# A four-layer graph network on one core: layer 2's feed-forward computed for all rows in small steps, instead of for packed rows in one stage

## The chip, the core and the metric

The kernel is written in Bass with the Tile framework and runs on one core of a Trainium2 chip. The metric is the device time of one execution in microseconds (us). A core has engines that run side by side, each with a queue of its own that it works off in order: PE (TensorE, matrix products; its weight loads are shown as PEld), DVE (VectorE), ACT (ScalarE), POOL (GpSimd) and SP (SyncE, which issues most DMA transfers). They wait for one another through semaphores. Which instruction stands where in a queue is fixed when the kernel is built.

## What is computed

3125 nodes with 256 features and 50,000 edges go through four layers. Each adds a graph convolution and a mixing block to the rows, and then a feed-forward block. The change concerns layer 2's feed-forward, what stands before it and what follows it:

```python
x = x + L2_gnn(xn, edge_index, ...) + L2_mix(xn[None], ...)[0]   # attention with 8 heads; linear attention
x = x + L2_ffn(_layernorm(x)[None], ...)[0]
xn = _layernorm(x)
x = x + L3_gnn(xn, ..., edge_index) + L3_mix(xn[None], ...)[0]

def L2_ffn(x, wr, br, w1, b1, w2, b2):            # b = 1, s = 3125
    weights = (jnp.einsum('bsd,do->bso', x, wr) + br)[..., 0]
    k = max(1, int(0.5 * s)); kk = k - 1          # kk = 1561
    _, idx = jax.lax.top_k(weights, k)
    sel_idx = idx[:, :kk]
    sel = jnp.take_along_axis(x, sel_idx[:, :, None], axis=1)
    h = jax.nn.gelu(jnp.einsum('bkd,dh->bkh', sel, w1) + b1, approximate=True)   # 256 -> 1024
    y = jnp.einsum('bkh,hd->bkd', h, w2) + b2                                    # 1024 -> 256
    y = y * jnp.take_along_axis(weights, sel_idx, axis=1)[..., None]
    return jnp.zeros_like(x).at[batch_idx, sel_idx].set(y) + x
```

So each row gets a weight; the 1561 rows with the largest weights are kept; only they go through the feed-forward, whose result is multiplied with the weight and added.

## The kernel before

The rows are held on chip as `x`, 25 tiles of 128 rows (`NB = 25`), handled in groups of `BB = 5` tiles. Most of the kernel is emitted through Tile, whose pools decide when a buffer is free again; the order on each queue is the order in which the Python code emits.

*End of layer 2's attention* (`gat`, from L906). For each group of five tiles: scale by the softmax sums, add the bias (L917), statistics (`stats`: L441 and L442 on DVE, a square root at L444 on ACT), shift and scale (L922, five Identity activations on ACT), multiply with `gamma` (L923), add to `x` (L924).

*Feed-forward* (`ffn2`). The weights `w1` and `w2` (1024 KB each) are loaded. `norm_x` normalises all groups; its `each` copies the normed rows to `xn_all` (L1784) and makes each row's weight `wt` (L1787). A search over the bits of the weights follows: eight rounds of four bits, each with a comparison on DVE (L1833), a count (L1835), a sum over partitions on PE (L1837) and a choice. From its threshold come `sel`, the kept rows, `cw`, the factor of each row, and by three prefix sums (`before`, L1856 and L1857) the place `ids` of each kept row and the place `back` where each row finds its result. Then 25 indirect DMAs on POOL write every tile's rows to their places in DRAM (`kept`, L1890). The first 13 tiles of it, `KS`, are the kept rows: SP loads them (`xs`, L1903), PE transposes them (`to_T`, L456, copied by ACT or DVE at L457), and the feed-forward runs in groups of four tiles: eight chunks of 128 hidden features (`feat`, L502, 512 columns; gelu on ACT, L1913), then for each tile the second product (`tok`, L465, with the bias at L463), a copy (L1918) and a store to DRAM (`done`, L1919). Last, 25 indirect DMAs on POOL gather each row's result (`yb`, L1923), and DVE adds it times `cw` to `x` (L1926).

*Layer 3* (`layer3`, `dense3`). After the index set-up of its mixture of experts, the kernel reads a flag (`unfit`) and takes, for these inputs, `dense3`: norm by groups, and in `first` the normed rows times `di` are split into three bf16 parts `ha` by casts on ACT (L2139) and subtractions on DVE (L2141). The graph product is then, for each of 25 blocks of destinations, 75 products of `ha` with a matrix of edge counts (`product`, L2154). The first of them needs the last `ha`.

`layer2`, `ffn2` and `layer3` follow one another in the list of layers in `tile_gps`; `xT`, the transposed rows, is one buffer up to layer 2 and another in layer 3.

Of the kernel before, what the change touches and what calls it, by code (L numbers as in the profile page):

```python
# [19 lines left out]
P = 128  # L20
N = 3125
D = 256
# [18 lines left out]
NR = 40  # L41
RB = 4
# [22 lines left out]
class Net:  # L65
# [671 lines left out]
    def gat(self, pool, pre, H, tiny, side, deg=None, after=None, during=None):  # L737
# [169 lines left out]
        then = after() if after is not None else None  # L907
        for b in range(0, NB, BB):
            s = slice(b, b + BB)
            if H > 4 or b < 2 * BB:  # L910
                nc.vector.tensor_tensor(heads[:, s], heads[:, s], bc(ws[:, s], [None, None, None, C]), ALU.mult)
            else:
                for t in range(b, b + BB):
                    for h in range(H):
                        nc.scalar.mul(heads[:, t, h, :], heads[:, t, h, :], ws[:, t, h:h + 1])
            o = agg[:, s, :D]
            nc.vector.tensor_tensor(o, o, bc(bias, [None, BB, None]), ALU.add)  # L917
            mv, rs = self.stats(pool, lambda i: agg[:, b + i, :D], BB, "gat")
            off = pool.tile([P, BB], F32, name="off")
            nc.vector.scalar_tensor_tensor(off, mv[:, :, 0], -1.0, rs, op0=ALU.mult, op1=ALU.mult)  # L920
            for i in range(BB):
                nc.scalar.activation(o[:, i, :], o[:, i, :], AF.Identity, bias=off[:, i:i + 1], scale=rs[:, i:i + 1])  # L922
            nc.vector.tensor_tensor(o, o, bc(gamma, [None, BB, None]), ALU.mult)  # L923
            nc.vector.tensor_tensor(self.x[:, s], self.x[:, s], o, ALU.add)  # L924
            if then is not None:
                then(b)
# [379 lines left out]
    def mixture(self, whole, mark, pre, names, kind, gate, gate_b, H, act, twice=False, affine=None):  # L1306
# [103 lines left out]
        def rest():  # L1410
# [8 lines left out]
            with self.pool("own_ps", 1, PSUM) as few:  # L1419
# [26 lines left out]
                place = p.tile([1, ES], F32, name="place")  # L1446
# [147 lines left out]
    def layer0(self):  # L1594
        with ExitStack() as whole:
            rest = []

            def after():
# [5 lines left out]
                return lambda b: all(True for _ in route(b))  # L1604
# [152 lines left out]
    def layer2(self):  # L1757
        nc, tc = self.nc, self.tc
        self.norm_x()
        with self.pool("mix", 1) as mw:  # L1760
            with self.pool("gnn", 1) as gw, self.pool("gnn2", 2) as gp:
                self.gat(Pools(gw, gp, GAT_ONE), "L2_gnn_", 8, 0.0, lambda own: self.mix2(mw, own))

    def ffn2(self):
# [3 lines left out]
        KS = -(-keep // P)  # L1768
        pre = "L2_ffn_"
        done = self.dram.tile([KS * P, D], F32, name="done")  # L1770
        kept = self.dram.tile([(KS + NB) * P, D], F32, name="kept")
        with self.pool("kept", 1) as p:
            w1, w2 = self.weight(p, pre + "w1"), self.weight(p, pre + "w2")
            b1, b2 = self.plain(p, pre + "b1"), self.three_of(p, pre + "b2")
            xn_all = p.tile([P, NB, D], F32, name="xn_all")

            none = p.tile([P, D], F32, name="none")
            nc.vector.memset(none, 0.0)
            nc.sync.dma_start(kept[(KS - 1) * P:KS * P], none)
            wt = p.tile([P, NB], F32, name="wt")  # L1780
            wr, br = self.rows(p, pre + "wr"), self.rows(p, pre + "br")

            def each(lp, ps, b, xn):
                nc.scalar.copy(xn_all[:, b:b + BB, :], xn)  # L1784
                for i in range(BB):
                    junk = lp.tile([P, D], F32, name="junk")
                    nc.vector.scalar_tensor_tensor(junk, xn[:, i, :], 1.0, wr, op0=ALU.mult, op1=ALU.mult,  # L1787
                                                   accum_out=wt[:, b + i:b + i + 1])

            self.norm_x(keep_xn=True, each=each, turn=False)  # L1790
            nc.vector.tensor_scalar(wt, wt, br, None, op0=ALU.add)

            wk = p.tile([P, NB], F32, name="wk")
# [4 lines left out]

            ids = p.tile([P, NB], I32, name="ids")
            back = p.tile([P, NB], I32, name="backs")  # L1800
            cw = p.tile([P, NB], F32, name="cw")
            with self.pool("rk", 1) as r, self.pool("rk2", 2) as r2, \
                    self.pool("rk_ps", 2, PSUM) as ps:
# [23 lines left out]
                for sh in range(28, -4, -4):  # L1827
# [8 lines left out]
                    q = ps.tile([P, nd], F32, name="q")  # L1836
                    nc.tensor.matmul(q, self.ones, n, start=True, stop=True)  # L1837
                    d = r2.tile([P, nd], F32, name="d")
# [14 lines left out]
                def before(x, name):  # L1853

                    q = ps.tile([P, 2, NB], F32, name="qb")
                    nc.tensor.matmul(q[:, 0], self.earlier, x, start=True, stop=True)  # L1856
                    nc.tensor.matmul(q[:, 1], self.ones, x, start=True, stop=True)  # L1857
                    t = r.tile([P, NB], F32, name=name + "t")
                    nc.vector.tensor_copy(t, q[:, 1])
                    one = r.tile([P, NB], F32, name=name + "o")  # L1860
                    nc.vector.memset(one, 0.0)
                    run = r.tile([P, NB], F32, name=name + "r")
                    nc.vector.tensor_tensor_scan(run, t, one, 0.0, ALU.add, ALU.add)
                    pl = r.tile([P, NB], F32, name=name + "p")
                    nc.vector.tensor_tensor(pl, run, t, ALU.subtract)
                    nc.vector.tensor_tensor(pl, pl, q[:, 0], ALU.add)
                    return pl, run[:, NB - 1:]

                _, larger = before(both[:, 0], "l")
                place, _ = before(both[:, 1], "e")  # L1870
                want = r.tile([P, 1], F32, name="want")
                nc.vector.tensor_scalar(want, larger, -1.0, float(keep), op0=ALU.mult, op1=ALU.add)
# [3 lines left out]
                nc.vector.tensor_tensor(cw, sel, wt, ALU.mult)  # L1876
                place, _ = before(sel, "s")

                at = r.tile([P, NB], F32, name="at")
                nc.vector.tensor_tensor(at, place, sel, ALU.mult)  # L1880
                nc.vector.tensor_copy(back, at)
                node = r.tile([P, NB], F32, name="node")
                nc.gpsimd.iota(node, pattern=[[P, NB]], base=KS * P, channel_multiplier=1,
                               allow_small_or_imprecise_dtypes=True)
                nc.vector.tensor_tensor(place, place, node, ALU.subtract)
                nc.vector.tensor_tensor(place, place, sel, ALU.mult)
                nc.vector.tensor_tensor(place, place, node, ALU.add)
                nc.vector.tensor_copy(ids, place)
            for t in range(NB):
                s = nc.gpsimd.indirect_dma_start(  # L1890
                    out=kept, out_offset=bass.IndirectOffsetOnAxis(ap=ids[:, t:t + 1], axis=0),
                    in_=xn_all[:, t, :], in_offset=None)
                if t:
                    tc.declare_no_dep(s.ins, group=pre, reason="every row has a place of its own")
                tc.add_to_no_dep_group(pre, s.ins)

            with self.pool("ks", 1) as k1, self.pool("ks2", 2) as k2, \
                    self.pool("ks_ps", 2, PSUM) as ps:
                xs = k1.tile([P, KS, D], F32, name="xs")
                sT = k1.tile([P, 2, KS * P], F32, name="sT")  # L1900
                for t0 in range(0, KS, 4):
                    n = min(4, KS - t0)
                    nc.sync.dma_start(xs[:, t0:t0 + n, :],  # L1903
                                      kept[t0 * P:(t0 + n) * P].rearrange("(t p) f -> p t f", p=P))
                    for t in range(t0, t0 + n):
                        self.to_T(ps, xs[:, t, :], sT[:, :, t * P:(t + 1) * P])
                for t0 in range(0, KS, 4):
                    n = min(4, KS - t0)
                    h = k2.tile([P, 8, 512], F32, name="h")
                    for c in range(8):  # L1910
                        q = ps.tile([P, 512], F32, name="h")[:, :n * P]
                        self.feat(q, sT, t0 * P, n * P, w1, c * P)
                        nc.scalar.activation(h[:, c, :n * P], q, AF.Gelu_apprx_tanh, bias=b1[:, c:c + 1])  # L1913
                    y = k2.tile([P, 4, D], F32, name="y")
                    for i in range(n):
                        q = ps.tile([P, D], F32, name="y")
                        self.tok(q, h, i, w2, bias=b2)
                        nc.vector.tensor_copy(y[:, i, :], q)  # L1918
                    nc.sync.dma_start(done[t0 * P:(t0 + n) * P].rearrange("(t p) f -> p t f", p=P), y[:, :n, :])  # L1919
            with self.pool("co", 8) as g:  # L1920
                for t in range(NB):
# [525 lines left out]
```

## Time and profile before

| | |
|---|---|
| median of three runs | 6186.31 us (6184.32 to 6188.53) |
| the profiled execution | 6189.69 us, span 6187.9 us |
| mean granted clock of PE | 0.862 |
| PE busy | 4643.9 us (75%) |
| DVE busy | 3297.2 us (53%) |
| ACT busy | 1567.8 us (25%) |
| POOL busy | 2397.0 us (39%) |
| end of layer 2's attention to the scatter | 4182.3 to 4301.8 us |
| scatter, packed feed-forward, gather | 4301.8 to 4476.8 us |
| layer 3's norm, to the first product with the last `ha` | 4476.8 to 4527.0 us |

The profile records one execution. The span is the time between its first and last recorded instruction; the rest of the execution's own time, some 2 us, lies around it. Busy shares of the engines overlap, so they don't add up to the span. A clock of 1.00 is full speed of TensorE; the share granted is given for each stretch of time.

### The profile page before, as it was taken

The page shows a single profiled execution, that of the slowest core. Times are in us where ns is not written, and L with a number is a line of the kernel's source. Part 1 is how long each engine was busy: PE and PEld are TensorE (multiplying, and loading weights), DVE is VectorE, ACT ScalarE, POOL GpSimd, SP SyncE. Part 2 cuts the span into 40 slices and gives each one's busy share as a digit, 9 for nine tenths or more (in the row PEclk, how much of TensorE's full clock was granted, in tenths as well). Part 3 has the DMA queues.
Part 4 walks back from the last instruction along what each step waited for, and adds up shares of the span by engine and source line. Part 5 has one row for each costly group of instructions (what it writes and reads, how often), then busy time and mean ns, then how long its engine had stood idle before and what let it go on. Part 6 is the DMA issues. An engine that isn't in the chain of part 4 may idle for free.

```text
span 6187.9 us, 81932 instructions
## 1 busy us (share of the span) xinstructions
PE 4643.9 (75%) x25310; PEld 3283.6 (53%) x25310; DVE 3297.2 (53%) x8633; ACT 1567.8 (25%) x4108; POOL 2397.0 (39%) x2340
## 2 busy tenths in 40 slices
PE   1848775696778766656697758880699999997997
PEld 1314343583565344443683235550456888786996
DVE  6448777426798388876326567776142100134222
ACT  1213233222100245432222123311144201111332
POOL 1537774322777275552423567771100000011111
PEclk9969887797897777777798879995899999998998
DMA  2744442553333144332564324430111322124554
GB/s 82 220 122 117 118 120 66 179 177 102 93 97 102 55 151 137 130 117 66 160 184 131 99 72 123 120 116 27 57 62 65 131 99 73 59 96 153 182 172 160
DMA packets 385095, 710.60 MB, mean 115 GB/s; under 512 B 100817, under 2 KB 223256, under 8 KB 384652
## 3 DMA queue, kind: packets, MB, share of 16 engines
q1 hardware_dynamic: 266431, 425.79, 21.6%
q0 software_dynamic: 108064, 269.63, 14.9%
q10 hardware_dynamic: 10157, 9.80, 0.5%
q8 instruction: 213, 3.49, 0.2%
q14 instruction: 230, 1.88, 0.1%
HBM read 571.51 MB, written 133.47 MB: 114 GB/s over the span
## 4 chain that ended last, share of the span: by engine, by line
PE 43%; issue 17%; DVE 15%; POOL 11%; DMA 8%; ACT 3%; DVEq 2%; SPq 1%; ACTq 0%; another core or an unknown queue 0%; POOLq 0%
PE dn L2154 13%; PE mm L465 6%; POOL msg L531 6%; PE g L585 4%; PE g L862 3%; DMA msg<-L_gnn_htab,src 2%; PE h L1507 2%; PE y L1520 2%; DVE ohd L2085 2%; POOL ase L531 2%; DVE agg L544 2%; DMA terms<-outr 2%; POOL back L1524 1%; PE mm L2214 1%; PE mm L2098 1%
## 5 line engine op out<-in xcount | busy, mean ns | idle before, releaser
L531 POOL DMA_INDIRECT msg<-L_gnn_c_tab,src x832 | 827.4, 995 | 606.6 <-issue 225.3
L531 POOL DMA_INDIRECT msg<-L_gnn_htab,src x832 | 887.5, 1067 | 383.5 <-issue 213.0
L544 DVE TENSOR_TENSOR agg<-agg,g 128x256 f32 (+2 forms) x1664 | 697.6, 419 | 215.0 <-PE g L862 96.3
L2154 PEld LDWEIGHTS <-a 128*128 128x128 bf16 x7500 | 736.2, 98 | 116.9 <-issue 28.3
L862 PE MATMUL g<-msg,oh 128*128 128x261 f32 (+1 forms) x1664 | 568.7, 450 | 194.0 <-DVE agg L544 176.5
L1402 POOL DMA_INDIRECT sent<-xs,ids x150 | 153.0, 1020 | 1292.9 <-DMA yb<-done,backs 1036.3
L585 PE MATMUL g<-msg,oh 128*128 128x256 f32 x1664 | 581.6, 484 | 86.5 <-DMA msg<-L_gnn_c_tab,src 35.5
L862 PEld LDWEIGHTS g<-msg,oh 128*128 128x128 f32 x1664 | 314.2, 211 | 433.6 <-DVE agg L544 328.2
L585 PEld LDWEIGHTS g<-msg,oh 128*128 128x128 f32 x1664 | 358.5, 238 | 235.4 <-DVE oh L566 86.8
L1524 POOL DMA_INDIRECT back<-y,toi x168 | 163.6, 974 | 787.1 <-DVE y L1523 510.6
L1507 PE MATMUL h<-xe,w 128*128 128x128 f32 x3584 | 436.8, 278 | 5.3 <-DMA w<-in_L_ffn_W 5.2
L2154 PE MATMUL dn<-ha,a 128*128 128x256 bf16 x3750 | 428.5, 275 | 7.7 <-ACT ha L2139 6.5
L1520 PE MATMUL y<-w,hT 128*128 x1792 | 431.2, 388 | 0.0
L1511 ACT ACTIVATE hT<-h,br 128x128 f32<-128x128 f32 x896 | 256.4, 369 | 669.5 <-issue 573.4
L1507 PEld LDWEIGHTS h<-xe,w 128*128 128x128 f32 x3584 | 422.0, 195 | 7.0 <-DVE toi L1496 6.2
L2154 PE MATMUL dn<-hb,a 128*128 128x256 bf16 x3750 | 418.2, 273 | 0.0
L1520 PEld LDWEIGHTS y<-w,hT 128*128 128x128 f32 x1792 | 326.5, 190 | 57.0
L1523 DVE COPY y<-y 128x256 f32<-128x256 f32 x168 | 71.2, 424 | 521.7 <-PE y L1520 521.5
L851 DVE TENSOR_TENSOR msg<-msg,alpha 128x1024 f32<-128x1024 f32 x208 | 254.1, 1222 | 133.4 <-DMA msg<-L_gnn_htab,src 119.9
L819 ACT COPY stage<-dm 128x24 bf16 (+1 forms) x832 | 182.5, 220 | 452.1 <-PE pd L825 281.6
L531 POOL DMA_INDIRECT ase<-tab,src x208 | 231.8, 1115 | 148.4 <-PE q L657 85.3
L566 DVE TENSOR_SCALAR oh<-cols,dl,ew 128x128 f32<-128x128 f32 x832 | 266.6, 350 | 0.0
(730 smaller groups left out, 7155.0 us busy)
## 6 DMA issues: line engine op xcount, KB each, us to landing
a<-counted SPq DMA_DIRECT2D x100, 800.0 KB
w<-in_L_ffn_W SPq DMA_DIRECT2D x128, 512.0 KB
w<-in_L_ffn_W SPq DMA_DIRECT2D x64, 1024.0 KB
counted<-T SPq DMA_DIRECT2D x40, 800.0 KB
dr<-dl_rows SPq DMA_DIRECT2D x104, 256.0 KB
sent<-zeros SPq DMA_DIRECT2D x25, 1040.0 KB
xr<-sent SPq DMA_DIRECT2D x168, 130.0 KB
lw<-lo_rows SPq DMA_DIRECT2D x78, 256.0 KB
```

Source lines behind the costliest of these rows:

```text
L465: nc.tensor.matmul(q, xT[:, k, t * P:(t + 1) * P], w[:, k, cols], start=(k == 0 and bias is None), stop=(k == nk - 1))
L531: self.nc.gpsimd.indirect_dma_start(out=out, out_offset=None, in_=table, in_offset=bass.IndirectOffsetOnAxis(ap=self.src[:, t:t + 1], axis=0))
L544: self.nc.vector.tensor_tensor(at, at, q, ALU.add)
L566: nc.vector.tensor_scalar(oh[:, j, :], self.cols, self.dl[:, t:t + 1], self.ew[:, t:t + 1], op0=ALU.is_equal, op1=ALU.mult)
L585: self.nc.tensor.matmul(r, oh[:, j, :], msg[j], start=True, stop=True)
L851: nc.vector.tensor_tensor(mh, mh, bc(al_, [None, None, None, C]), ALU.mult)
L862: nc.tensor.matmul(q, oh[:, j, :], msg[:, j, :], start=True, stop=True)
L1507: nc.tensor.matmul(q[:, i, :], d["w1"][:, k, c * P:(c + 1) * P], d["xe"][:, k, :], start=(k == 0), stop=(k == 1))
L1511: nc.scalar.activation(hT[:, c, :], q[:, i, :], act, bias=d["br"][:, c:c + 1])
L1520: nc.tensor.matmul(q, d["hT"][:, c, :], w2f[:, bass.ds(e * (nh * D) + c * D, D)], start=False, stop=(c == nh - 1))
L1524: s = nc.gpsimd.indirect_dma_start(out=self.back, out_offset=bass.IndirectOffsetOnAxis(ap=d["to"][:, 0:1], axis=0), in_=y, in_offset=None)
L2154: nc.tensor.matmul(q, a[:, k, :], h[:, k, i, :], start=(k == 0 and i == 0), stop=(k == NB - 1 and i == 2))
```

## The change

The feed-forward is no longer a stage between a packing and an unpacking of rows. It is made for all 25 tiles (25 x 128 rows instead of 13 x 128), from the transposed rows `xT`, and the result of a row that isn't kept is multiplied by a factor of zero (`f_cw`). The work is a Python generator, `forward()`, which emits one small step whenever it is asked to: for a pair of tiles four steps of two chunks of hidden features (256 columns each, gelu over 128x256 on ACT), then one step for each tile's second product.

- *The first 14 tiles* (`FIRST`) are emitted from `between()`: four calls in each group of the attention's end, two in each group of the norm, which now follows its attention group directly (`each(b)`), and two in each round of the search. What is left of them comes after the last round. Their results are copied by ACT to `ys`, and added once `f_cw` is known (`add_kept`).
- *The last 11 tiles* are emitted by `later()` within layer 3's norm, 6, 6, 6, 18 and 0 steps behind its five groups, with the weights loaded a second time; their results are added from PSUM.
- The scatter, `xs`, the transposes of packed rows, `done` and the gather go, with the prefix sum that gave the places. The transposes of layer 3's rows move out of its norm and behind the steps of their group, since the steps still read `xT`. `xT` is one buffer for the whole kernel.
- The index set-up of layer 3's mixture moves ahead of layer 2. The loads of the first feed-forward weights move ahead of the attention's end.

The core of the diff (pools and the like are left out, and the removed code that stands in the listing above):

```diff
+FIRST = 14
+PAIRS = [(t, 2) for t in range(0, 24, 2)] + [(24, 1)]
...
-        then = after() if after is not None else None
+        then, between = after() if after is not None else (None, None)
+        between = between or (lambda: None)
...
+            between()
             nc.vector.tensor_tensor(o, o, bc(bias, [None, BB, None]), ALU.add)
             mv, rs = self.stats(pool, lambda i: agg[:, b + i, :D], BB, "gat")
             off = pool.tile([P, BB], F32, name="off")
             nc.vector.scalar_tensor_tensor(off, mv[:, :, 0], -1.0, rs, op0=ALU.mult, op1=ALU.mult)
             for i in range(BB):
                 nc.scalar.activation(o[:, i, :], o[:, i, :], AF.Identity, bias=off[:, i:i + 1], scale=rs[:, i:i + 1])
+            between()
             nc.vector.tensor_tensor(o, o, bc(gamma, [None, BB, None]), ALU.mult)
+            between()
             nc.vector.tensor_tensor(self.x[:, s], self.x[:, s], o, ALU.add)
+            between()
             if then is not None:
...
     def layer2(self):
-        nc, tc = self.nc, self.tc
+
         self.norm_x()
-        with self.pool("mix", 1) as mw:
-            with self.pool("gnn", 1) as gw, self.pool("gnn2", 2) as gp:
-                self.gat(Pools(gw, gp, GAT_ONE), "L2_gnn_", 8, 0.0, lambda own: self.mix2(mw, own))
-
-    def ffn2(self):
+        with ExitStack() as whole:
+            then = []
+
+            def after():
+                each, between, rest = self.ffn2(whole)
+                then.append(rest)
+                return each, between
+
+            with self.pool("mix", 1) as mw:
+                with self.pool("gnn", 1) as gw, self.pool("gnn2", 2) as gp:
+                    self.gat(Pools(gw, gp, GAT_ONE), "L2_gnn_", 8, 0.0, lambda own: self.mix2(mw, own), after=after)
+            then[0]()
...
+    def forward(self, w1, w2, b1, b2, hp, ps, units, put):
+
+        nc = self.nc
+        for t0, n in units:
+            h = []
+            for half in range(2):
+                h.append(hp.tile([P, 4, 2 * P], F32, name="hf", bufs=3))
+                for c in range(0, 4, 2):
+                    q = ps.tile([P, 512], F32, name="mm")
+                    for j in range(2):
+                        f = (4 * half + c + j)
+                        r = q[:, j * n * P:(j + 1) * n * P]
+                        self.feat(r, self.xT, t0 * P, n * P, w1, f * P)
+                        nc.scalar.activation(h[half][:, c + j, :n * P], r, AF.Gelu_apprx_tanh, bias=b1[:, f:f + 1])
+                    yield
+            for i in range(n):
+                q = ps.tile([P, 512], F32, name="mm")[:, :D]
+                nc.tensor.matmul(q, self.ones3, b2, start=True, stop=False)
+                for c in range(8):
+                    nc.tensor.matmul(q, h[c // 4][:, c % 4, i * P:(i + 1) * P], w2[:, c, :], start=False, stop=(c == 7))
+                put(t0 + i, q)
+                yield
...
+    def add_kept(self, t, y):
+        self.nc.vector.scalar_tensor_tensor(self.x[:, t, :], y, self.f_cw[:, t:t + 1], self.x[:, t, :],
+                                            op0=ALU.mult, op1=ALU.add)
...
+        ys = p.tile([P, FIRST, D], F32, name="ys")
+        ready = [0]
+
+        def until(steps):
+            for t0, n in PAIRS:
+                if t0 < FIRST:
+                    for _ in range(4 + n):
+                        while ready[0] < t0 + n:
+                            yield
+                        next(steps)
+                        yield
+
+        steps = until(self.forward(w1, w2, b1, b2, p, ps, [u for u in PAIRS if u[0] < FIRST],
+                                   lambda t, q: nc.scalar.copy(ys[:, t, :], q)))
+
+        def between():
+            next(steps, None)
+
+        def each(b):
+            mv, rs = self.stats(lp, lambda i: self.x[:, b + i, :], BB, "ln")
+            between()
+            xs = []
+            for i in range(BB):
+                xn = lp.tile([P, D], F32, name="xn", bufs=8)
+                self.normed(xn, self.x[:, b + i, :], mv, rs, i)
+                xs.append(xn)
+            for i in range(BB):
+                self.to_T(ps, xs[i], self.xT[:, :, (b + i) * P:(b + i + 1) * P])
+                junk = lp.tile([P, D], F32, name="junk")
+                nc.vector.scalar_tensor_tensor(junk, xs[i], 1.0, wr, op0=ALU.mult, op1=ALU.mult,
+                                               accum_out=wt[:, b + i:b + i + 1])
+                nc.vector.tensor_tensor(self.x[:, b + i, :], self.x[:, b + i, :], xs[i], ALU.add)
+            ready[0] = b + BB
+            between()
...
                     nc.tensor.matmul(q, self.ones, n, start=True, stop=True)
+                    between()
+                    between()
...
+                for _ in steps:
+                    pass
...
-            for t in range(NB):
-                s = nc.gpsimd.indirect_dma_start(
-                    out=kept, out_offset=bass.IndirectOffsetOnAxis(ap=ids[:, t:t + 1], axis=0),
-                    in_=xn_all[:, t, :], in_offset=None)
...
-                for t in range(NB):
-                    y = g.tile([P, D], F32, name="yb")
-                    nc.gpsimd.indirect_dma_start(
-                        out=y, out_offset=None, in_=done,
-                        in_offset=bass.IndirectOffsetOnAxis(ap=back[:, t:t + 1], axis=0))
-                    nc.vector.scalar_tensor_tensor(self.x[:, t, :], y, cw[:, t:t + 1], self.x[:, t, :],
-                                                   op0=ALU.mult, op1=ALU.add)
...
+            for t in range(FIRST):
+                self.add_kept(t, ys[:, t, :])
...
+    def later(self, own, ps):
+
+        p = own.enter_context(self.pool("kept", 1, side="right"))
+        w1, w2 = self.weight(p, "L2_ffn_w1"), self.weight(p, "L2_ffn_w2")
+        return self.forward(w1, w2, *self.forward_biases(p), p, ps, [u for u in PAIRS if u[0] >= FIRST], self.add_kept)
...
+                xns[b] = xn
...
+            with ExitStack() as own, self.pool("ln", 2) as lp:
+                steps = self.later(own, ps)
+                for g in range(NB // BB):
+                    self.norm_group(lp, ps, g * BB, each=first, turn=False)
+                    for _ in range((6, 6, 6, 18, 0)[g]):
+                        next(steps, None)
+                    xn = xns.pop(g * BB)
+                    for i in range(BB):
+                        t = g * BB + i
+                        self.to_T(ps, xn[:, i, :], self.xT[:, :, t * P:(t + 1) * P])
+            gp = more.enter_context(self.pool("dense2", 2))
...
-                self.norm_x(ps, each=first)
...
-        with net.pool("runs", 1) as net.rc, net.pool("xT", 1) as xp:
-            net.xT = xp.tile([P, 2, NP], F32, name="xT")
-            net.norm_x(keep_xn=True)
-            net.edges()
-            for f in (net.layer0, net.layer1, net.ffn1, net.layer2, net.ffn2):
-                f()
-        last = net.layer3()
-        next(last)
-        next(last)
+        with net.pool("xT", 1) as net.xp:
+            net.xT = net.xp.tile([P, 2, NP], F32, name="xT")
+            last = net.layer3()
+            with net.pool("runs", 1) as net.rc:
+                net.norm_x(keep_xn=True)
+                net.edges()
+                for f in (net.layer0, net.layer1, net.ffn1):
+                    f()
+                next(last)
+                net.layer2()
+            next(last)
```

## The prediction

> **What bounds the kernel now.** I read the page's clock row, then the windows over the stages that the change touches, then the timeline and the groups by form there. The page:
>
> ```profile
> span 6187.9 us, 81932 instructions
> PE   1848775696778766656697758880699999997997
> PEclk9969887797897777777798879995899999998998
> ```
>
> Forty slices of 155 us. From slice 30 on PE is nearly full; slice 27 (4177 to 4331 us) is the only one where PE is empty and the granted clock is half. The change works there and in slices 28 and 29. The windows, columns: window and length, then busy time of PE, weight loads, DVE, ACT, POOL (instructions), granted clock, DMA share, GB/s:
>
> ```profile
> 4182.30:4226.20 43.90, 0.00 (x0) 0.00 (x0) 39.39 (x80) 14.10 (x30) 0.00 (x0) 0.53 0.08 24
> 4226.20:4262.80 36.60, 0.00 (x0) 0.00 (x0) 36.07 (x148) 7.79 (x10) 0.44 (x3) 0.50 0.04 7
> 4262.80:4301.80 39.00, 8.34 (x30) 6.84 (x30) 27.26 (x137) 0.00 (x0) 0.00 (x0) 0.50 0.00 0
> 4301.80:4339.20 37.40, 0.00 (x0) 0.00 (x0) 0.00 (x0) 0.00 (x0) 24.39 (x25) 0.50 0.32 110
> 4339.20:4442.50 103.30, 100.29 (x373) 65.48 (x373) 7.55 (x18) 24.98 (x42) 0.00 (x0) 0.97 0.08 26
> 4442.50:4476.80 34.30, 0.00 (x0) 0.00 (x0) 12.01 (x26) 0.00 (x0) 23.95 (x25) 0.52 0.48 140
> 4476.80:4527.00 50.20, 29.38 (x179) 21.74 (x180) 43.01 (x108) 27.16 (x43) 0.00 (x0) 0.74 0.19 57
> ```
>
> Row by row: attention's end, the norm, the search, the scatter of rows, the feed-forward of 13 packed tiles, the gather back, layer 3's norm. Each stage has one engine and hands on to the next; PE works 138 of 345 us. Rows of the timeline (start, us, engine, line; in brackets the idle before and what ended it):
>
> ```profile
> 4301.83 1.03 POOL L1890 DMA_INDIRECT kept<-xn_all,ids  x1 [39.22 <-DVE ids L1888]
> 4366.23 3.72 PE L465 MATMUL y<-L_ffn_w,h 128*128 128x256 f32 x16
> 4442.58 0.98 POOL L1923 DMA_INDIRECT yb<-done,backs  x1 [109.05 <-DMA done<-y]
> 4526.97 3.15 PE L2154 MATMUL dn<-ha,a 128*128 128x256 bf16 x14 [2.44 <-ACT ha L2139]
> ```
>
> The first and third are hand-overs; the last is where layer 3's product gets its last operand, `ha`. Behind it PE is 100 of 100 us busy, so a shift of that operand is a shift of the end.
>
> **What goes.** Scatter 37.4, packed feed-forward 103.3, gather 34.3: 175.0 us of chain, all exposed. On POOL 50 indirect DMAs go; SP's loads of `xs` and stores of `done` go with them. POOL and SP have nothing else in these windows that would become late.
>
> **What comes: PE work.** Groups by form, 4140 to 4540 (busy, mean ns | idle before):
>
> ```profile
> L465 PE MATMUL y<-L_ffn_w,h 128*128 128x256 f32 x208 | 48.2, 384 | 0.0
> L502 PE MATMUL h<-sT,L_ffn_w 128*128 128x512 f32 x96 | 43.3, 602 | 0.0
> L1913 ACT ACTIVATE h<-h,L_ffn_b 128x512 f32<-128x512 f32 x24 | 16.5, 687 | 53.4 <-PE h L502 53.4
> ```
>
> The means overlap each other; the cadence is what counts: a run of 16 records with 256 columns took 3.72 us in the timeline (L465), 0.2325 us each. A pair of tiles now makes 32 such records for h (7.44 us) and twice 17 for y with the bias (2 x 3.86): 15.1 us. Fourteen tiles are 7 x 15.1 = 105.7, the last eleven 5 x 15.1 + 8 = 83.5, together 189 us instead of 91.5 (48.2 + 43.3). So PE gets some 97 us more, and the chain loses 175 plus whatever PE now does beside DVE.
>
> **Stage A, up to the kept rows.** The order on PE: group 0's transposes, then steps. Group 0 of x is normed after DVE's work on two groups' worth (about 15 us of tail and 13 of norm from 4182), so PE starts near 4211. From there at full clock: 105.7, transposes 25 x 0.45 = 11, the search's products 8 x 0.6 = 5: 122 us. DVE needs about 15.4 us a group (sum of its two tail rows: 75.5 / 5), PE 15.1 + 2.3: PE is the slower, DVE's tail hides beneath it. The search, 39 us alone, has 16 steps (40 us) put between its rounds: also beneath PE, but each round now stands in PE's queue behind two steps and each step's gelu. Stalls: ACT holds each group's two square roots, which wait for DVE's statistics, with the gelus queued behind them; four PSUM buffers (some 7 us of steps) absorb part. Bounds 0 to 6 us a group, taken 2.5: 10 us in all. Cold clock 4. End of A: 4211 + 122 + 14 = 4347; fourteen additions of `ys` of 0.36 us run beside it, the last near 4351.
>
> **Stage B, layer 3's norm with eleven tiles.** `later()` loads both weights again. w1 cannot start before stage A's buffers are free; 1 MB takes 3.3 us plus 2 for its start (estimated from the loads of that size for the experts, which came about 3.3 us apart between 5684 and 5718): a PE gap of 5.4, to 4356 with nothing else to run. Then 80.7 us of steps left after a first that runs beside it, 9 of transposes (now behind the steps, since xT is read by these), 3 cold, stalls 8 to 12 (same bounds): last y near 4472. The steps of group 3 (18) end before group 4's norm, since its additions need them. Behind the last y, in order: addition, statistics, square root with its table, norm, product with `di`, the addition of a bias row to all of x (6.8 us by L934, which now stands between on DVE), two casts of 1.26 on ACT and two subtractions of 1.48: 18.7 us. Last `ha` near 4490 against 4526.9: **-37 us**.
>
> **Small edits.** After that: the 6.8 us addition no longer comes later (-4); the first attention products of layer 3 stand behind 194 product records, before 145, but have fewer waits (-2). W1 and wqkv of layer 3 now load only after the last `ha`, where they came at 4441 before; 70 product records (7.7 us) cover a 3.3 us load, without that cover 3 to 5 us. Moving layer 3's index set-up ahead of layer 2: its DMAs stand on POOL among gathers of 1 us; none is awaited before layer 3; 0, at worst 3. The first weight load comes 50 us earlier, beside the last gathers: 0, at worst +3. Sum: -43. The profiled execution was 6189.7 (span 6187.9), the median 3.4 below: 6147 for a profiled run, **6144** for the median.
>
> **Two rules against the change.** First the clock. 4080 to 4180, where PE works in pieces, read:
>
> ```profile
> 4080.00:4180.00 100.00, 80.32 (x326) 50.35 (x326) 79.01 (x190) 15.56 (x55) 68.09 (x65) 0.90 0.38 111
> 4490.00:4527.00 37.00, 25.08 (x161) 18.37 (x162) 29.82 (x62) 20.63 (x30) 0.00 (x0) 0.82 0.14 50
> ```
>
> 80% busy got 0.90, 68% got 0.82; the long idle windows 0.50. The Trainium skill, "TensorE: Matmul & The Clock Gate", section "HAM oscillation — how this bites in real kernels", says why: idle gaps above about 3.4 us drop the clock by half. By the rule my 2.5 us stalls cost nothing beyond two warm-ups (7 us, what I booked); by the rows 0.90 on 218 us of PE work in A and B costs 24, so 17 more: 6161. I expect PE near 90% busy, above both rows, and keep the rule's sum; the row's goes into the range.
>
> Second the tables. In the instruction order gelu and square root alternate: 23 table loads on ACT between attention and layer 3's products instead of 3. The trace:
>
> ```profile
> 4345.22 1.28 ACT L1913 ACT_TABLE_LOAD   x1
> 4346.52 0.69 ACT L1913 ACTIVATE h<-h,L_ffn_b 128x512 f32<-128x512 f32 x1
> ```
>
> The gelu starts as the load ends: no more than its length. The Trainium skill, "ScalarE: Activation LUTs", section "What ACT_TABLE_LOAD costs", adds a drain: 2.66 us in all. ACT per tail group is five Identities 2.56, roots 0.6, copies 2.4, eight gelus (0.48 estimated between the 0.37 and 0.69 of 128 and 512 columns) 3.8 and four loads: 14.5 us by the row, 20 by the page. Against PE's 17.4 the first hides, the second binds and costs 2.6 a group, some 13 us in all: 6157. I take the row.
>
> **Rivals.**
> - *Full overlap*: neither stalls (20) nor the reload (5) nor cold clock (7) show: 6144 - 32 = 6112. For it: four PSUM buffers and three halves of h. Against: the in-order roots on ACT.
> - *Lock-step*: at each of 12 switched roots PE runs dry: root waits for DVE, DVE for an addition behind PE, 3.5 us each beyond my stalls on about ten: +35, 6180.
> - *Slower: the clock gate in the interleaved stages.* Stalls grow beyond the gate's window, so PE runs most of A and B half clocked. 218 us of work at 0.7 is 311: +86, less the 7 booked: 6223. It decides once the mean granted clock over 4211 to 4472 falls below 218 / (218 + 43 + 7) = 0.81; the row with 68% busy stood at 0.82. Against it: PE has a backlog of steps whenever a group is ready.
> - *Not what it says*: rows still packed or the other branch of layer 3 taken: 6186. The order of instructions has no scatter left, so little.
>
> **Numbers.** Forecast (6120 to 6168) 0.62; full overlap 0.13; lock-step (6165 to 6200) 0.15; clock gate 0.08; not what it says 0.02. Bounds of stalls (0 to 24 in A, 0 to 24 in B), clock (0 to 17) and tables (0 to 13) make 6110 to 6185, which leaves out the slower rival and part of two others. Runs differ by 0.07%; I call 0.2%, 12 us, the bound of no change. Faster: 0.62 + 0.13 + half of lock-step, 0.82; same 0.08; slower 0.08 + the end of lock-step, 0.10.
>
> **Signs.** No indirect DMA between 4182 and the first `dn<-ha`; PE 85 to 95% busy from 4211 to 4347 with a clock of 0.93 or more; the search's last round near 4340; one PE gap of 5 to 6 us ahead of the second weights; gelu rows 128x256 near 0.48; 23 table loads of 1.28; last `ha` cast near 4490 on the old axis. Wrong if PE gaps above 3.4 us stand at every group, if the window's clock is below 0.81, or if the end behind `dn<-ha` shifts by other than the last cast does.

## The result and the profile after

The changed kernel takes 6099.53 us (median of four runs, 6096.7 to 6100.59), the kernel before 6187.07 in the same comparison: ratio 0.9858, 95% interval 0.9841 to 0.9875. That is 87.5 us less, where 43 were forecast: 20 us below the forecast's own range (6120 to 6168), and 10 below the low end of all its bounds (6110). Its profiled execution took 6100.59 us.

The page of the changed kernel, with the rows that were shown of the kernel before:

```profile
span 6098.8 us, 82979 instructions
PE   1848776596777766656597938887999999996997
PEclk9969887697898677778698969898999999998998
```

The empty slice with the half clock is gone. The windows of the changed kernel, cut where the stages now begin and end (columns as before: length, busy time of PE, weight loads, DVE, ACT, POOL, granted clock, DMA share, GB/s):

```profile
4178.60:4206.20 27.60, 2.59 (x12) 2.14 (x11) 27.38 (x72) 7.24 (x17) 0.00 (x0) 0.60 0.01 0
4206.20:4319.00 112.80, 110.93 (x524) 91.79 (x522) 80.64 (x309) 62.64 (x121) 0.00 (x0) 0.99 0.00 1
4319.00:4327.80 8.80, 0.05 (x1) 0.05 (x1) 8.80 (x33) 2.18 (x4) 0.00 (x0) 0.78 0.46 147
4327.80:4419.80 92.00, 90.50 (x436) 73.59 (x437) 38.09 (x79) 45.77 (x77) 0.00 (x0) 0.98 0.10 36
4419.80:4439.70 19.90, 14.35 (x121) 11.71 (x120) 15.17 (x17) 8.42 (x14) 0.00 (x0) 1.00 0.05 13
```

Row by row: up to the first transposed group; stage A with 14 tiles; the second load of the weights; stage B with 11 tiles; the last group's norm down to the last `ha`. Before, PE was busy in 138 of 345 us here, and now in 218 of 261. PE does 80 us more, and these windows together are 84 us shorter.

For all comparisons below I use one *stretch*: from the start of the last product of the attention on PE to the start of the last `ha` cast on ACT. It is 345.7 us before and 259.8 after (4178.6 to 4438.4), -85.9. Ahead of it the two traces differ by 1.4 us, behind it by 1.8 (1662.2 and 1660.4 us to the end): 89.1 together, which is the difference of the spans. So nearly the whole gain lies in the stretch.

What PE waited for between 4205 and 4440 in the changed kernel (view of waits: in all, how often, the longest, in us):

```profile
PE mm L504 <- DMA L_ffn_w<-in_L_ffn_w: 8.8, 1, 8.8
PE dn L2196 <- ACT ha L2165: 4.7, 2, 2.4
PE mm L504 <- ACT hf L1793: 1.9, 3, 1.1
PE mm L1797 <- ACT hf L1793: 1.4, 2, 0.8
PE mm L458 <- DVE xn L451: 0.9, 1, 0.9
```

L504 is the first product, L1793 the gelu, L1797 the bias of the second product, L458 a transpose. In 205 us of steps PE waited 3.3 us for a gelu.

### The profile page after: what moved, and what is told of

Its sections match the earlier page's. It is cut to its first block, busy times and chain, and to the rows that moved or that the text cites. A ratio compares the mean times of both kernels' runs of the same rounds, so it can differ in the third digit from the quotient of the medians.

```text
span 6098.8 us, 82979 instructions
## 1 busy us (share of the span) xinstructions
PE 4728.5 (78%) x25818; PEld 3377.0 (55%) x25818; DVE 3292.5 (54%) x8630; ACT 1620.5 (27%) x4215; POOL 2345.7 (38%) x2289
## 4 chain that ended last, share of the span: by engine, by line
PE 45%; issue 17%; DVE 14%; POOL 11%; DMA 8%; ACT 3%; DVEq 2%; SPq 1%; ACTq 0%; another core or an unknown queue 0%; POOLq 0%
PE dn L2196 13%; PE mm L467 7%; POOL msg L533 5%; PE g L587 4%; PE g L864 3%; DMA msg<-L_gnn_htab,src 3%; PE h L1514 2%; PE y L1527 2%; PE mm L504 2%; DVE ohd L2111 2%; POOL ase L533 2%; DMA terms<-outr 2%; DVE agg L546 2%; PE mm L1799 1%; PE mm L2254 1%
## 6 DMA issues: line engine op xcount, KB each, us to landing
dr<-dl_rows SPq DMA_DIRECT2D x104, 256.0 KB
lw<-lo_rows SPq DMA_DIRECT2D x78, 256.0 KB
```

## The experiments

**Theory A**, formed from this profile: PE is the bound of both stages, as forecast, but it hardly ever waits for ACT, since four PSUM buffers let it run ahead of ACT's roots; the forecast put in waits, and prices of a half clock, that aren't there. **Theory B**: the gain comes from dropping scatter and gather, and the order of the steps matters little. **Theory C**: the table loads on ACT still bind.

| run | stretch, us | ratio to before (95%) |
|---|---|---|
| changed kernel | 259.8, again 260.4 | 0.9858 (0.9841 to 0.9875), again 0.985 (0.9837 to 0.9863) |
| no steps in the attention's end | 302.0 | 0.9929 (0.9914 to 0.9944) |
| two PSUM buffers | 276.4 | 0.9889 (0.9874 to 0.9905) |
| gelu left out | 252.6 | 0.9849 (0.9836 to 0.9862) |
| `ys` apart | 262.9 | 0.9856 (0.9841 to 0.9871) |
| addition split | 256.0 | 0.9836 (0.9801 to 0.9871) |
| 10 tiles first | 280.9 | 0.9897 (0.9871 to 0.9924) |
| `ys` apart, first pair ahead | 258.4 | 0.9873 (0.9838 to 0.9907) |
| that and the split addition | 254.6 | 0.9867 (0.9838 to 0.9895) |
| 16 tiles first | 258.4 | 0.9859 (0.9844 to 0.9873) |
| the best: `ys` apart, first pair ahead, split addition, `b1` and `di` early | 247.9 | 0.9838 (0.9824 to 0.9852) |

The chips differ: the four runs from "addition split" to "that and the split addition" were on one where the kernel before takes 6846 us, with wider intervals. The stretch hardly depends on that: the second run of the changed kernel, on another chip, differs by 0.6 us, and with the addition split the kept rows are known 138.4 us into the stretch, as in the changed kernel (138.1). The changed kernel itself was not run on the slower chip. So small effects are read from the stretch, though each is one profiled execution, and 1 or 2 us show little.

A gain in the stretch is not always one of the whole. From the start of the last cast to the start of the last product with `ha` it takes 887.4 us in the changed kernel and 887.8 in its second run, but 890.5 to 890.8 with the gelu left out and in the two runs with the split addition and the first pair ahead: 3 us of their gain come back there. In these three PE waits 1.2 to 2.0 us for layer 3's `wqkv`, for which it doesn't wait in the changed kernel; but with the addition split alone it waits 1.4 us too and takes 887.4, so the cause of the 3 us stays open.

### No steps in the attention's end

```diff
         def between():
-            next(steps, None)
+            pass
```

> The calls between() emit nothing; all steps of the first 14 tiles are emitted behind the search's products (the scheduler may still move them up within the search). Nothing is left out. Theory A (PE is the bound of both stages and the gain comes from filling it while DVE ends the attention and norms): PE starts the steps at about 4267 instead of 4206, the 106 us of products end near 4378 instead of 4319, so +57 us against the changed kernel: about 6157. Theory B (the gain comes from dropping scatter and gather alone, where the steps stand matters little): at most 6120.

The stretch is 302.0 us, +42.2, and the ratio rises from 0.9858 to 0.9929. Theory B falls in its size: without the steps under the attention's end half of the gain is lost, and half stays. Theory A had +57. The first second-product stood 85.1 us behind the last attention product instead of 35.3: 50 us later, where theory A had taken 61 for the start. The kept rows were known at 112.5 us of the stretch instead of 138.1, and the second weights cost PE 6.3 us instead of 8.8.

### Two PSUM buffers

```diff
-        ps = whole.enter_context(self.pool("kept_ps", 4, PSUM))
+        ps = whole.enter_context(self.pool("kept_ps", 2, PSUM))
```

> Two PSUM buffers instead of four for the first 14 tiles and their transposes; nothing is left out. Theory A (the four buffers are what keeps PE busy while ACT stands at a root, so my 2.5 us of stall per group were avoided by them): each of eight switched roots (1.28 + 0.30 + 1.28 us on ACT) shows on PE by 1 to 2 us, +8 to +16, so 6108 to 6116, and PE rows with ACT hf as the one waited for. Rival (roots don't reach PE because of where the scheduler puts them, not because of the buffers): 6097 to 6103.

276.4, +16.6, just above what theory A expected, and all of it in stage A: the kept rows were known at 154.8 instead of 138.1. ACT's timeline in the changed kernel shows what stands ahead of a gelu at each root (start, us, engine, line):

```profile
4214.80 1.28 ACT L446 ACT_TABLE_LOAD   x1
4216.10 0.30 ACT L446 ACTIVATE lnrs<-lnmv,eps 128x5 f32<-128x5 f32 x1
4216.41 1.28 ACT L1793 ACT_TABLE_LOAD   x1
4217.71 0.47 ACT L1793 ACTIVATE hf<-mm,L_ffn_b 128x256 f32<-128x256 f32 x1
```

A switch to the root and back holds ACT for 2.9 us. A buffer holds 1.86 us of PE's work (8 records of 0.2325), and the buffer that ACT still reads is no use to PE. So by this estimate PE can run on through three buffers, 5.6 us, where there are four, and through one, 1.9 us, where there are two: the first reaches over the switch, the second doesn't. PE's timeline with two buffers, its windows there, and its waits for gelus in the stretch (changed kernel: 3.3 in all):

```profile
4229.09 2.86 PE L504 MATMUL mm<-xT,L_ffn_w 128*128 128x256 f32 x12 [2.24 <-ACT hf L1793]
4234.19 0.26 PE L1797 MATMUL mm<-f_b,ones 3*128 3x256 bf16 x1 [2.24 <-ACT hf L1793]
...
4274.32 0.91 PE L504 MATMUL mm<-xT,L_ffn_w 128*128 128x256 f32 x3 [2.24 <-ACT hf L1793]
```

```profile
4230.00:4236.00 6.00, 3.76 (x15) 2.75 (x14) 6.00 (x17) 5.91 (x10) 0.00 (x0) 0.88 0.00 0
4236.00:4242.00 6.00, 6.00 (x24) 4.72 (x24) 6.00 (x17) 1.77 (x3) 0.00 (x0) 0.84 0.00 0
```

```profile
PE mm L504 <- ACT hf L1793: 6.8, 5, 2.2
PE mm L1797 <- ACT hf L1793: 2.2, 1, 2.2
```

For the second of these waits ACT began its switch at 4230.75, and PE stood from 4231.95. Here is the forecast's wait of 2.5 us a group, in size though not in every group, and the clock falls to 0.84 with it. Of the 16.6 us some 9 are waits (11.1 in stage A with those for copies, instead of 1.9), and some 7 are PE's own records, which took 117.7 us of stage A instead of 110.9. ACT switched less often here (18 table loads instead of 22), so it isn't the number of switches. The scheduler did order ACT otherwise than in the changed kernel; what that alone does is not separated from the buffers.

### Gelu left out

```diff
-   nc.scalar.activation(h[half][:, c + j, :n * P], r, AF.Gelu_apprx_tanh, bias=b1[:, f:f + 1])
+   nc.scalar.activation(h[half][:, c + j, :n * P], r, AF.Identity, bias=b1[:, f:f + 1])
```

> Leaves the gelu out: Identity in its place in layer 2's feed-forward, which shares a table with the square root, so some 20 table loads of 1.28 us go from ACT; all else stays. Theory A (the loads lie under PE's work): 6094 to 6100, PE's stalls of about 4 us in all are the most that can go. Theory C (the loads or a drain behind them bind, 13 to 26 us): 6073 to 6087.

252.6, -7.2, of which 2.6 in stage A (kept rows known at 135.5 instead of 138.1). In the trace of the changed kernel 22 loads of 1.283 us stand in these stages on ACT, 28 us. PE's 3.3 us of waits for gelus are gone, and what it waits for `ha` falls from 4.7 us to 1.6; a new wait comes behind the stretch:

```profile
PE mm L963 <- DMA L_mix_wqkv<-in_L_mix_wqkv: 2.0, 1, 2.0
PE dn L2196 <- ACT ha L2165: 1.6, 2, 1.2
```

From the last attention product to the last product with `ha` it is 1143.1 us instead of 1147.2 (again 1148.2): 4 to 5 us, near theory A's bound of 4. The ratios don't tell the two kernels apart. So about three quarters of the loads or more are hidden, and theory C falls in its size, but the loads aren't free.

### `ys` apart from the weights

```diff
+        kp = whole.enter_context(self.pool("kept3", 1, side="right"))
...
-        ys = p.tile([P, FIRST, D], F32, name="ys")
+        ys = kp.tile([P, FIRST, D], F32, name="ys")
```

> ys and the other small tiles get a pool of their own, so that the second load of w1 overlays the first w1 and not ys; nothing is left out. In the changed kernel SP stands at that load until DVE has added the 14 tiles of ys (4322.6) and PE then waits 8.8 us for it. Theory A (that wait is on the path): the load starts with the end of the last h product, some 7 us earlier, and 5 to 8 us of the gap go: 6091 to 6095. Rival (layer 3's first norm, or the reading of the branch flag, would hold PE just as long): 6098 to 6101.

262.9, +3.1: nearer to the rival, which had named layer 3's first norm. The load did start earlier and PE no longer waits for it, but the wait only changed its name. In this kernel, between 4320 and 4360, PE waited for one thing:

```profile
PE mm L504 <- ACT hf L1793: 10.9, 1, 10.9
```

Its ACT at that place:

```profile
4342.18 1.26 ACT L2166 CAST ha<-v 128x1280 bf16<-128x1280 f32 x1 [3.89 <-DVE v L2175]
4343.35 0.30 ACT L446 ACTIVATE lnrs<-lnmv,eps 128x5 f32<-128x5 f32 x1
4343.66 1.28 ACT L1793 ACT_TABLE_LOAD   x1
4344.95 0.47 ACT L1793 ACTIVATE hf<-mm,L_ffn_b 128x256 f32<-128x256 f32 x1
```

The first gelu stands behind layer 3's first cast, which waits for DVE, and behind a second root.

### The bias addition split

```diff
-            self.add_rows(mz, "L3_gnn_b3", pre + "bo")
+            s = self.rows(mz, "L3_gnn_b3")
+            self.nc.vector.tensor_add(s, s, self.rows(mz, pre + "bo"))
+            for t in range(NB):
+                self.nc.vector.tensor_tensor(self.x[:, t, :], self.x[:, t, :], s, ALU.add)
```

> The addition of layer 3's two bias rows to all of x (6.82 us in one instruction on DVE, 4427.4, between the last group's product with di and its two subtractions) is cut into 25 instructions of one tile; nothing is left out. Theory A (end of stage B is a chain of DVE and ACT, and this instruction stands in it for about 5.5 us beyond the cast it waits for anyway): the stretch from the last attention product to the last ha cast goes from 259.8 to about 254, ratio to the kernel before 0.985. Rival (the product records that PE has left cover it): no change, 0.9858.

256.0, -3.8. DVE in the changed kernel, with the instruction that stood in the way:

```profile
4425.94 1.49 DVE L2174 TENSOR_TENSOR v<-xn,di 128x1280 f32<-128x1280 f32 x1
4427.35 6.82 DVE L941 TENSOR_TENSOR x<-x,L_gnn_b_rows 128x6400 f32<-128x6400 f32 x1
4434.09 1.48 DVE L2167 TENSOR_TENSOR v<-v,ha 128x1280 f32<-128x1280 f32 x1
```

In pieces most of it fits into DVE's waits for the casts.

### 10 tiles, and 16 tiles, before the search's end

```diff
-FIRST = 14
+FIRST = 10
...
-                    for _ in range((6, 6, 6, 18, 0)[g]):
+                    for _ in range((9, 9, 12, 17, 0)[g]):
```

> 10 tiles before the search's end and 15 behind it instead of 14 and 11; nothing is left out. Theory A (PE's work bounds both stages, so only its sum counts): within 4 us of the changed kernel, stretch 256 to 264, the kept rows known some 12 to 25 us earlier. Rival (stage A is bound by DVE's tail and search, so work taken out of it makes PE idle there and is paid in full later): stretch about 285, ratio 0.990.

280.9, +21.1: theory A falls in the form in which it was put. The kept rows were known only 7.6 us earlier (130.5), and what follows became 28.7 us longer, about the price of four tiles (30). Stage A has a chain of its own, attention's end, norm and search; with fewer steps PE idles beside it. It waited 15.4 us there for DVE's part of the search (`n`, 13.0, and `both`, 2.4), and 11.4 for the second weights instead of 8.8. With 16 (the four numbers then 4, 4, 4, 17):

> 16 tiles before the search's end and 9 behind it (one scratch buffer of DVE instead of two, to make room); nothing is left out. With 10 tiles the stretch grew by 21 us, because stage A then has less PE work than its chain on DVE is long (about 112 us without any steps) and PE idles. Theory A2 (at 14 both stages are bound by PE, so two tiles moved to A lengthen it by 15 and shorten B by 15): 257 to 263. Rival (B has a chain of its own on DVE and ACT as well, so it does not get shorter): 270 to 276.

258.4, -1.4. So at 14 and at 16 both stages are PE's, and at 10 the chain on DVE is the longer.

### The first pair ahead of layer 3's norm

On top of `ys` apart; the second hunk orders group 0's root behind the pair's last gelu. Group 3 then has 11 steps behind it instead of 18.

```diff
+                for _ in range(6):
+                    next(steps)
+                self.behind = self.gelu
...
+            self.tc.add_manual_dep(root.ins, self.behind.ins.name, ...)   # in stats()
```

> As the run with ys apart, where the wait for w1 went but PE then stood 10.9 us for ACT, whose first gelu was queued behind two roots and a cast of layer 3's norm. Here the first pair of the last 11 tiles is emitted ahead of that norm, and its root is ordered behind the pair's eight gelus on ACT; nothing is left out. Theory (the gap had two waits one behind the other, the reload and the ACT queue): both gone, the stretch 259.8 goes to 250 to 254, ratio 0.9845 to 0.985. Rival (the delayed norm of group 0 comes back at the end): 258 to 264.

258.4: 4.5 less than with `ys` apart alone, 1.4 less than the changed kernel. It fell into the rival's range. With the split addition:

> The last run and the split addition together; nothing is left out. If the two are on the path one behind the other their gains add: stretch 245 to 249, ratio 0.9835 to 0.984, faster than both kernels of this case.

254.6, short of the expected 245 to 249, and only 1.4 us less than the split addition alone. A third wait had taken the place, in that kernel's ACT:

```profile
4979.97 0.23 ACT L2167 ACTIVATE di<-di 128x25 f32<-128x25 f32 x1 [1.93 <-DVE di L2166]
4982.26 1.28 ACT L1801 ACT_TABLE_LOAD   x1 [2.07 <-DMA L_ffn_b<-in_L_ffn_b]
```

The root of `di` waits for DVE's additions, and then the gelu's bias, 4 KB, is issued on SP behind w2, which waits for the last second product.

### The best version

```diff
+        b1 = self.plain(self.xp, "L2_ffn_b1")      # loaded once, kept for stage B
+        self.di = di = self.xp.tile([P, NB], F32, name="di")   # made here, not in dense3
```

> The best so far (ys apart, first pair ahead of layer 3's norm, split addition), and what held the first gelu then: its bias b1 was loaded behind w2, and the factors di stood ahead of it on ACT behind the 14 additions on DVE. b1 stays in a buffer of its own and di is made before the attention's end; nothing is left out. Theory (PE's gap of 5 us between the stages goes): stretch 248 to 251, ratio 0.9835 to 0.9845, faster than the changed kernel by some 10 us. Rival (the delayed norm of group 0 or the weights themselves hold PE): 253 to 256.

247.9, 11.9 less than the changed kernel, at the low end of what was expected. To the last product with `ha` it is 8.5 us less (1138.7 instead of 1147.2). All that PE still waits for between 4215 and 4435 there:

```profile
PE mm L1805 <- ACT hf L1801: 2.4, 3, 0.8
PE dn L2210 <- ACT ha L2176: 2.1, 2, 1.5
PE mm L509 <- ACT hf L1801: 1.2, 3, 0.5
PE mm L463 <- DVE xn L456: 1.1, 1, 1.1
```

On this chip its median is 6097.71 us, the changed kernel's 6107.6, the kernel's before 6199.32. The intervals of the two ratios (0.9824 to 0.9852 and 0.9837 to 0.9863) overlap, so the gain over the changed kernel rests on the two traces.

## Why the prediction was right in direction and wrong in size

Right: the direction, PE as the bound of both stages, and the path (the last `ha` came 87 us earlier and the end 89). The rows that were foretold came: no indirect DMA, 22 table loads instead of 23, a gelu of 0.474 us (0.48 estimated), one gap for the second weights. The sizes; times of the changed kernel are on its own axis, on which the attention ends 1.4 us earlier:

| term | predicted, us | measured, us |
|---|---|---|
| PE starts the steps at | 4211 | 4206.2 |
| stage A, to its last second product | 136 | 112.8 |
| from there to the last second product of stage B | 125 | 100.8 |
| end chain, to the end of the last cast | 18.7 | 19.9 |
| last `ha` ready at | 4490 | 4439.7 |
| gain behind it | 6 | 1.8 |

- **The step that failed is the waits**: "taken 2.5: 10 us in all" for stage A and "stalls 8 to 12" for stage B. A further 13 us sat in stage B's sum without a name: 4356 and the terms listed give 4459, not 4472, and what they stood for is not on record. That is 33 us of waits; PE waited 3.3 us for gelus, 1.9 in stage A and 1.4 in stage B. It is the greater part of the 47 us by which the two stages came out shorter (213.6 instead of 261). The four buffers were named and then not worked out: three of them free, 5.6 us of PE's work, against a switch of 2.9 us. The run with two buffers puts 16.6 us back, with waits of 2.24 us.
- **Cold prices in a warm stage.** Transposes "25 x 0.45" and search products "8 x 0.6" are durations at a clock of 0.50 (the kernel before had five tiles in 2.37 us and a round in 0.61). At full clock, in the changed kernel's timeline:

```profile
4222.22 1.34 PE L458 MATMUL mm<-ident,xn 128*128 128x128 f32 x10
4273.83 0.29 PE L1904 MATMUL q<-n,ones 128*128 128x15 f32 x2
```

  That is 0.27 us a tile and 0.29 us a round. Group 0's transposes also lie ahead of the start that the sum counts from. Together some 8 us of the 23 in stage A and 4 of the 24 in stage B, with 7 more booked for the clock of which little came. So the 218 us of PE work put into A and B were too much as well: 201.5 were measured there. That the windows above add up to 218 is chance, since they take in 17 us outside A and B.
- **The clock.** Row and rule were weighed, and the rule kept. In stages A and B the clock was 0.99 and 0.98, so the rows' 17 us would have been wrong: they were taken where PE was 80 and 68% busy, and here it was 98%. The rule of the Trainium skill ("TensorE: Matmul & The Clock Gate", section "HAM oscillation — how this bites in real kernels"), that PE should have no idle gaps above about 3.4 us, was enough here with waits for gelus of up to 1.1 us. With two buffers it was not: gaps of 2.24 us close to one another, none longer behind the first transposes, took the clock from 0.98 to 0.88 and 0.84 in successive windows of 6 us.
- **The tables.** Row and not page, as taken: in the rows above each load is followed by its activation within 0.02 us, with no drain between. "Hides" was a little too much: without the loads the stretch is 7.2 us shorter, and 4 to 5 us of that are left at the last product with `ha`.
- **The second weights**: 9 us from the end of A (additions to 4351, then 5.4), 8.8 measured. SP issued the load at 4322.68, when DVE had added `ys`, whose place it takes, and PE went on 5.1 us later. But behind that wait stood others, 10.9 us for ACT with `ys` apart and 5.2 with the first pair ahead, so "nothing else to run" wasn't the whole of it.
- **Stage A hides the search**: true at 14 tiles. With 10 the chain on DVE decides, which the forecast's one sum for PE didn't contain.
- **Rivals.** Full overlap (6112) was nearest, and even it was too slow, since it kept the cold prices and the 13 us without a name; it also took off the reload, which did show. Lock-step needs PE to run dry at each root; even two buffers put back only 16.6 us. The clock gate did not come.
- **Slips in the sums**, none of which decides: 75.5 / 5 is 15.1 us of DVE a group, not 15.4; the clock gate's 7 us are taken off twice (6230, not 6223); the bounds at their upper ends give 6202, not 6185.

## What to carry to other kernels

Before a wait is priced, work out how far the waiting engine can run ahead: the buffers that are free, so one fewer than there are, times the work that each holds, against the longest thing that its supplier does in between. Take prices from rows at the clock that the new stage will have, not at the clock of the stage that it replaces. Where one gap has several waits behind one another, removing the one that the trace names gains little until the last is gone: the stretch grew by 3.1 us with `ys` apart alone; with the first pair ahead too it shrank by 1.4; and beside the split addition, with `b1` and `di` out of the way as well, it shrank by 8.1 (256.0 to 247.9), of which 3.4 came back behind it.

## What was not expected

The order on a queue is not simply that of the code; what was said on that ahead of the prediction is wrong. The framework's scheduler moves instructions within what the data allow: with `between()` empty, steps emitted behind the search were spread through it again; the bias addition, emitted behind the casts, came ahead of two subtractions. The runs with the first pair ahead put the gelus before the root by an explicit dependency; none was made without it. Making the roots on DVE, so that ACT keeps one table, was not tried and stays open; the run without gelu suggests 4 to 5 us at most from the table loads.
